# Reciprocal square roots on GpSimd's power operation, outside layer 1

## The chip, the cores and the metric

The kernel runs on one core of a Trainium2 chip. The metric is the device time of one execution in microseconds. A core has five engines, each with a queue of its own that is worked through in order: PE (TensorE, matrix products; PEld is its loading of weights), DVE (VectorE), ACT (ScalarE, which applies functions by table), POOL (GpSimd) and SP (SyncE, which here issues most DMAs). Engines meet only at semaphores and at the data in the on-chip memories.

## The reference

The input x is one image of 256 channels by 64 x 64 pixels in float32, that is 4096 tokens of 256 channels. Four layers follow each other, each a residual on x.

- Layer 0: group norm without scale, then linear attention over sliding windows with 8 heads of 32 channels: q and k are sigmoids, v is divided by its norm, and the sums over three windows are divided by q times the windowed k.
- Layer 1: group norm, then a deformable 3 x 3 convolution with a layer norm, offsets and masks.
- Layer 2: layer norm, then causal gated linear attention in which k and v are divided by their norms; then layer norm and a mixture of 8 experts, two for each token.
- Layer 3: layer norm, softmax attention of all 4096 tokens with each other; then layer norm and a mixture of 8 wider experts, two for each token.

The lines that the change bears on are the norms:

```python
v = v / jnp.maximum(jnp.linalg.norm(v, axis=1, keepdims=True), 1e-12)   # layer 0

def _l2_normalize(x, axis=-1):                                          # layer 2: k and v
    n = jnp.sqrt(jnp.sum(x * x, axis=axis, keepdims=True))
    return x / jnp.maximum(n, 1e-12)

def _ln_t(v, eps=1e-5):                                                 # layers 2 and 3, attention and experts
    m = jnp.mean(v, axis=-1, keepdims=True)
    s = jnp.var(v, axis=-1, keepdims=True)
    return (v - m) / jnp.sqrt(s + eps)
```

## The kernel before, in words

Tokens lie in 32 tiles of 128 (P = 128, NT = 32), four tiles to a block of 512 (TPB = 4, NB = 512, NBLK = 8 blocks). A framework for tiles puts the operations of each engine into an order of its own before the program runs, from its own estimates and the dependences, and places the semaphores. Only the tensor engine's order in the main part of layer 0 is written out by hand. Buffers come from pools and rotate.

An inverse norm is made the same way everywhere: a small tile of sums of squares or of variances gets a floor or an epsilon added on VectorE, then ScalarE takes the square root in place, then VectorE the reciprocal in place. ScalarE evaluates a function from a table, and a function that is not in the table at hand has an ACT_TABLE_LOAD in front of it, which the profile counts to the line of the function. There are these places:

- `layer_norm` (L188): statistics of up to four tiles (L195, L196), L198 adds epsilon, L199 and L200 are the square root and the reciprocal on 128 x 4 elements (`ln_rstd`), and L208 applies it on VectorE; with `on_act` ScalarE does. It is called by `attn2_project` (L1151), by `route` (L1594) and by layer 3's first stage (L1886).
- `project0` (L345): the projections of layer 0. It runs for each half of the channels. The products for q and k come first; then, for each of 8 blocks, products for k and v (in PSUM, `l_kv_ps`), a sigmoid for k on ScalarE (L367), a square of v (L369), the sum over each head's 32 channels (L370), the floor (L371), the square root and reciprocal of 128 x 16 elements `l_ss` (L372, L373), the product with v (L376), and the states k times v (L144, `l_S_ps`), copied out by L382. After a half, `sums0` (L384) adds the states over windows on POOL, and `norms0` (L403) computes the windowed k times q on VectorE (L429 to L437) with one product for each step on PE (L439). The scheduler mixes the steps of `norms0` with the next half's blocks.
- `attn2_project` (L1142): for each of 8 blocks, `layer_norm`, transposes (`to_channels`, L217), the products for q, k and v, a product q times k on POOL (L1163), the squares of k and v on ScalarE (L1170) with the sums on VectorE (L1171), the floor (L1172), the square root and the reciprocal of 128 x 64 elements `a_ss` (L1173, L1174), the product with v on VectorE (L1175) and with k on POOL (L1176), then transposes of v and the products for the gate. Most of its buffers exist once (`bufs=1`).
- `attn2_sum` (L1278): the causal sums of layer 2, two tiles at a time, with the masks (L1307) on VectorE and the products L1332 on PE. Between them run the steps of `route` (L1585) for the block before: `layer_norm`, the addition and a copy on POOL (L1596, L1597), the logits, the choice of two experts (L1579 is the exponential of its softmax), the places of the tokens in the experts' lists (L1633 to L1636), and eight indirect DMAs on POOL's queue that scatter the rows (L1639).
- Layer 3's attention: a stage of norms for all blocks (L1886), which waits for the gathered results of the experts of layer 2; then, for each block of queries, 32 tiles of keys with scores, an exponential (L1938) and products with v (L1943), and one step of `route` after every fourth tile of keys.
- `rstd` (L146) for group norms and for layer 1, and a general path of layer 2 (L1426) that is not executed on these inputs.

Of the kernel before, what the change touches and what calls it, by code (L numbers as in the profile page):

```python
# [10 lines left out]
F32 = mybir.dt.float32  # L11
BF16 = mybir.dt.bfloat16
I32 = mybir.dt.int32
AF = mybir.ActivationFunctionType
ALU = mybir.AluOpType
# [4 lines left out]
P = 128  # L20
# [58 lines left out]
def bc(ap, axis, n):  # L79

    ap = ap.unsqueeze(axis)
    shape = list(ap.shape)
    shape[axis] = n
    return ap.to_broadcast(shape)


class Net:
# [6 lines left out]
    def constants(self, pool):  # L94
        nc = self.nc
        self.ident = pool.tile([P, P], F32, tag="ident", name="ident")
        make_identity(nc, self.ident)
        self.ones_row = pool.tile([1, P], F32, tag="ones_row", name="ones_row")
        nc.gpsimd.memset(self.ones_row, 1.0)
        self.one = pool.tile([P, 1], F32, tag="one", name="one")  # L100
        nc.gpsimd.memset(self.one, 1.0)
        self.ones_col = self.one

        self.flags = pool.tile([P, 3], F32, tag="flags", name="flags")
        self.mom = pool.tile([P, 2, 2], F32, tag="mom", name="mom")

        self.grp = pool.tile([P, 16, 8], F32, tag="grp", name="grp")
        nc.gpsimd.memset(self.grp, 0.125)
        nc.gpsimd.affine_select(out=self.grp, in_=self.grp, pattern=[[-8, 16], [0, 8]], base=0,
                                channel_multiplier=1, compare_op=ALU.is_ge, fill=0.0)  # L110
        nc.gpsimd.affine_select(out=self.grp, in_=self.grp, pattern=[[8, 16], [0, 8]], base=7,
                                channel_multiplier=-1, compare_op=ALU.is_ge, fill=0.0)
        self.pp = pool.tile([P, NPP], F32, tag="pp", name="pp")
        nc.sync.dma_start(out=self.pp, in_=self.A["pp"])
# [31 lines left out]
    def rstd(self, pool, var, eps, tag):  # L146
# [5 lines left out]
        nc.vector.reciprocal(r, r)  # L152
        return r

    def group_norm(self, x, dst):


        nc, tc = self.nc, self.tc
        with tc.tile_pool(name="gn", bufs=1) as pool:
            mv = pool.tile([P, 2, 2], F32, tag="mv", name="gn_mv")  # L160
            for m in range(2):
                st = pool.tile([P, NBLK, 6], F32, tag=f"st{m}", name="gn_st")
                for j in range(NBLK):
                    nc.vector.bn_stats(st[:, j, :], x[:, m, j * NB : (j + 1) * NB])
                nc.vector.bn_aggr(mv[:, m, :], st)
            mean, r = self.group_scale(pool, mv)
            for m in range(2):
                for out, src in dst(m):
                    nc.vector.tensor_scalar(out, src, mean[:, m : m + 1], r[:, m : m + 1], ALU.subtract, ALU.mult)
# [18 lines left out]
    def layer_norm(self, pool, x, out, eps, on_act=False):  # L188

        nc = self.nc  # L190
        n = x.shape[1]
        st = pool.tile([P, TPB, 6], F32, tag="ln_st", name="ln_st")[:, :n]
        mv = pool.tile([P, TPB, 2], F32, tag="ln_mv", name="ln_mv")[:, :n]
        for i in range(n):
            nc.vector.bn_stats(st[:, i, :], x[:, i, :])  # L195
            nc.vector.bn_aggr(mv[:, i, :], st[:, i, :])  # L196
        r = pool.tile([P, TPB], F32, tag="ln_rstd", name="ln_rstd")[:, :n]
        nc.vector.tensor_scalar_add(r, mv[:, :, 1], eps)  # L198
        nc.scalar.activation(r, r, AF.Sqrt)  # L199
        nc.vector.reciprocal(r, r)  # L200
        if on_act:
            shift = pool.tile([P, TPB], F32, tag="ln_shift", name="ln_shift")[:, :n]
            nc.vector.scalar_tensor_tensor(shift, mv[:, :, 0], -1.0, r, ALU.mult, ALU.mult)
        for i in range(n):
            if on_act:
                nc.scalar.activation(out[:, i, :], x[:, i, :], AF.Identity, bias=shift[:, i : i + 1], scale=r[:, i : i + 1])
            else:
                nc.vector.tensor_scalar(out[:, i, :], x[:, i, :], mv[:, i, 0:1], r[:, i : i + 1], ALU.subtract, ALU.mult)  # L208
# [136 lines left out]
    def project0(self, hf, y, q, k, v, S, wp, ps):  # L345

        nc, w = self.nc, self.w
        for dst, base in ((q, 0), (k, C)):
            cols = slice(base + hf * P, base + hf * P + P)
            for nb in range(NBLK):  # L350
                p = ps.tile([P, NB], F32, tag="qk", name="l0_qk_ps")
                self.mm(p, [(w["w_qk0"][:, kt, cols], y[:, kt, nb * NB : (nb + 1) * NB]) for kt in range(2)])
                nc.scalar.activation(dst[:, nb * NB : (nb + 1) * NB], p, AF.Sigmoid)
        cols = slice(hf * 2 * P, (hf + 1) * 2 * P)
        for nb in range(NBLK):
            ts = slice(nb * TPB, (nb + 1) * TPB)
            kt4 = wp.tile([P, TPB, P], F32, tag="kt", name="l0_kt")
            ss = wp.tile([P, TPB, 4], F32, tag="ss", name="l0_ss")
            sq = wp.tile([P, TPB, 4, D], F32, tag="sq", name="l0_sq")
            ps_v = []  # L360
            for i in range(0, TPB, 2):
                p = ps.tile([P, 2, 2, P], F32, tag="kv", name="l0_kv_ps", bufs=4)
                for j in range(2):
                    t = nb * TPB + i + j
                    self.mm(p[:, j].rearrange("p a c -> p (a c)"),
                            [(y[:, kt, t * P : (t + 1) * P], w["w_kv0"][:, kt, cols]) for kt in range(2)])
                nc.scalar.activation(kt4[:, i : i + 2, :], p[:, :, 0, :], AF.Sigmoid)  # L367
                ps_v.append(p[:, :, 1, :].rearrange("p t (h c) -> p t h c", c=D))
                nc.scalar.activation(sq[:, i : i + 2], ps_v[-1], AF.Square)  # L369
            nc.vector.tensor_reduce(ss, sq, AX.X, ALU.add)  # L370
            nc.vector.tensor_scalar_max(ss, ss, 1e-24)  # L371
            nc.scalar.activation(ss, ss, AF.Sqrt)  # L372
            nc.vector.reciprocal(ss, ss)  # L373
            for i, p in zip(range(0, TPB, 2), ps_v):
                vs = v[:, nb * TPB + i : nb * TPB + i + 2, :].rearrange("p t (h c) -> p t h c", c=D)
                nc.vector.tensor_mul(vs, p, bc(ss[:, i : i + 2], 3, D))  # L376
            p = ps.tile([P, TPB, P], F32, tag="S", name="l0_S_ps", bufs=1)
            for i in range(TPB):
                self.mm(p[:, i, :], [(kt4[:, i, :], v[:, nb * TPB + i, :])])
            for h in range(4):  # L380
                hp = slice(h * D, (h + 1) * D)
                (nc.scalar.copy if h % 2 else nc.vector.tensor_copy)(S[hp, ts, :], p[hp, :, hp])  # L382
# [759 lines left out]
    def attn2_project(self, b, t, A, wg_bd, wp, ps):  # L1142

        nc, w = self.nc, self.w
# [22 lines left out]
        ss = wp.tile([P, 2, TPB, NH], F32, tag="ss", name="a2_ss")  # L1167
# [2 lines left out]
            nc.scalar.activation(sq, x, AF.Square)  # L1170
            nc.vector.tensor_reduce(ss[:, j], heads(sq), AX.X, ALU.add)  # L1171
        nc.vector.tensor_scalar_max(ss, ss, 1e-24)  # L1172
        nc.scalar.activation(ss, ss, AF.Sqrt)  # L1173
        nc.vector.reciprocal(ss, ss)  # L1174
        nc.vector.tensor_mul(heads(v), heads(v), bc(ss[:, 1], 3, D))  # L1175
        nc.gpsimd.tensor_tensor(heads(k), heads(k), bc(ss[:, 0], 3, D), ALU.mult)  # L1176
        vT = A["vT"][:, :, b * NB : (b + 1) * NB]
# [202 lines left out]
    def attn2_chunks(self, t, ctxt, sim, gate):  # L1380

        nc, tc, w, A = self.nc, self.tc, self.w, self.A
        with (
# [16 lines left out]
            for b in range(NBLK):  # L1400
# [21 lines left out]
                ss = wp.tile([P, TPB, 2 * NH], F32, tag="ss", name="a2_ss")  # L1422
                nc.vector.tensor_reduce(ss, heads(sq), AX.X, ALU.add)
                nc.vector.tensor_scalar_max(ss, ss, 1e-24)
                nc.scalar.activation(ss, ss, AF.Sqrt)
                nc.vector.reciprocal(ss, ss)  # L1426
                nc.vector.tensor_mul(heads(kv), heads(kv), bc(ss, 3, D))

                qT = wp.tile([P, 2, NB], F32, tag="qT", name="a2_qT")
# [776 lines left out]
```

## Time and profile before

| | us |
|---|---|
| median of three runs | 4277.86 |
| the three runs | 4275.56, 4277.86, 4278.22 |
| the profiled execution | 4303.36 |
| its span, first to last instruction | 4301.6 |
| layer 0, projections (65 to 230) | 165 |
| layer 2, projections (2000 to 2240) | 240 |
| layer 2, sums with routes (2280 to 2600) | 320 |
| layer 3, attention (2760 to 3710) | 950 |

The span is one execution as the hardware profiler recorded it, and all times of single instructions come from it. In the timeline's rows a start and a duration in microseconds are followed by the engine, the line, the operation, what is written and read, and in brackets how long the engine had stood idle before it and whose work ended that. In the rows of groups the busy time in microseconds and the mean of one instruction in nanoseconds stand after the first bar, and the idle time before them after the second. The mean granted clock of TensorE in this execution is 0.917 of full speed. The profile has 104 ACT_TABLE_LOAD instructions of 1283 ns each.

### The profile page before, as it was taken

To read this page: it belongs to the slowest core of one execution; us is meant where nothing else is said; L and a number is where in the kernel's file an instruction comes from. 1 tells how busy PE (TensorE), PEld (TensorE's weight loads), DVE (VectorE), ACT (ScalarE), POOL (GpSimd) and SP (SyncE) were. 2 spreads that over 40 slices of the span, in tenths; PEclk is the share of its full clock that TensorE was granted. 3 is DMA by queue.
4 is the path that set the end of the run, shared out by engine and by line. 5 is a ranking of instruction groups with operands and counts; after the bars stand their busy time and mean duration, and the time that the engine had idled before them with its cause. 6 is when DMAs were issued, how large, how long until landed. Compare 5 with 4: busy or idle time off the path is not lost.

```text
span 4301.6 us, 55879 instructions
## 1 busy us (share of the span) xinstructions
PE 3561.6 (83%) x21872; PEld 2318.2 (54%) x21872; DVE 1731.6 (40%) x3780; ACT 1254.4 (29%) x2172; POOL 1459.4 (34%) x1376
## 2 busy tenths in 40 slices
PE   7867888888877676675658779799999999899997
PEld 4412333322332465564436557566666668688886
DVE  6865445555554355455655555501001111211111
ACT  5423232333332353431111123322122222233331
POOL 1167776676775134433333334000000001011110
PEclk9989999999998888887768879899999999899999
DMA  1003313301001411110000157200000000355454
GB/s 49 2 25 103 111 58 92 95 21 35 19 23 67 120 54 45 44 54 16 0 0 21 40 169 251 87 0 10 10 11 10 11 5 16 118 191 196 182 203 167
DMA packets 137783, 294.00 MB, mean 68 GB/s; under 512 B 14817, under 2 KB 72802, under 8 KB 128290
## 3 DMA queue, kind: packets, MB, share of 16 engines
q1 hardware_dynamic: 113138, 234.80, 16.6%
q0 software_dynamic: 13056, 35.93, 2.2%
q10 hardware_dynamic: 11312, 19.55, 1.3%
q8 instruction: 177, 2.90, 0.3%
q14 instruction: 100, 0.82, 0.1%
HBM read 202.53 MB, written 87.70 MB: 67 GB/s over the span
## 4 chain that ended last, share of the span: by engine, by line
PE 33%; issue 11%; DVE 4%; DMA 3%; POOL 2%; ACT 1%; another core or an unknown queue 0%; SPq 0%; POOLq 0%; ACTq 0%; DVEq 0%
PE a_o_ps L1943 10%; PE a_s_ps L144 10%; PE f_h_ps L144 2%; PE a_qkv_ps L144 2%; PE f_y_ps L144 2%; POOL ys L1780 2%; DMA ys<-f_y,f_at 1%; PE a_q_ps L144 1%; PE a_o_ps L144 1%; DMA f_g<-ys 1%; PE tr_ps L217 1%; PE a_c_ps L1332 1%; DVE a_sm L1307 1%; PE a_u_ps L144 1%; PE a_st_ps L144 0%
## 5 line engine op out<-in xcount | busy, mean ns | idle before, releaser
L561 POOL TENSOR_TENSOR l_sm<-l_sc,mask 128x512 f32<-128x512 f32 (+3 forms) x624 | 783.8, 1275 | 285.4 <-ACT l_sc L555 278.2
L561 DVE TENSOR_TENSOR l_sm<-l_s,mask 128x512 f32<-128x512 f32 (+3 forms) x624 | 451.7, 747 | 475.2 <-PE l_s L547 472.9
L547 PE MATMUL l_s<-l_q,l_k 32*128 32x384 f32 (+2 forms) x3584 | 420.8, 538 | 199.1 <-DVE l_sm L561 187.6
L555 ACT COPY l_sc<-l_s 128x512 f32<-128x512 f32 (+3 forms) x448 | 339.0, 757 | 755.7 <-PE l_s L547 725.5
L1943 PE MATMUL a_o_ps<-a_v,a_e 128*128 128x257 f32 x2048 | 489.4, 380 | 0.0
L144 PE MATMUL a_s_ps<-a_qT,a_nT 128*128 128x512 f32 (+1 forms) x1152 | 487.8, 546 | 0.0
L1943 PEld LDWEIGHTS a_o_ps<-a_v,a_e 128*128 128x128 f32 x2048 | 388.9, 190 | 147.3 <-issue 104.1
L547 PEld LDWEIGHTS l_s<-l_q,l_k 32*128 32x128 f32 x3584 | 152.9, 192 | 464.6 <-DVE l_sm L561 276.1
L1639 POOL DMA_INDIRECT xs<-f_n,f_to x64 | 62.4, 976 | 883.9 <-DVE f_to L1636 841.1
L1938 ACT ACTIVATE a_e<-a_s_ps 128x512 f32<-128x512 f32 (+1 forms) x288 | 158.0, 549 | 687.4 <-PE a_s_ps L144 666.0
L144 PE MATMUL f_h_ps<-f_xT,f_w 128*128 128x256 f32 x1440 | 344.0, 387 | 11.9 <-DVE f_xT L1743 3.5
L1780 POOL DMA_INDIRECT ys<-f_y,f_at x144 | 139.6, 970 | 567.2 <-ACT f_y L1779 541.4
L144 PE MATMUL f_y_ps<-f_w,f_h 128*128 128x256 f32 x1440 | 328.1, 379 | 0.0
L144 PEld LDWEIGHTS f_h_ps<-f_xT,f_w 128*128 128x128 f32 x1440 | 265.0, 191 | 79.8 <-ACT f_h L1753 16.5
L852 PE MATMUL l_acc_ps<-ident,l_pr 128*128 128x128 f32 x1600 | 207.2, 290 | 118.7 <-DVE l_pr L848 114.3
L144 PEld LDWEIGHTS a_s_ps<-a_qT,a_nT 128*128 128x128 f32 x1152 | 216.3, 190 | 129.9 <-issue 112.9
L144 PEld LDWEIGHTS f_y_ps<-f_w,f_h 128*128 128x128 f32 x1440 | 268.2, 190 | 33.7
L852 PEld LDWEIGHTS l_acc_ps<-ident,l_pr 128*128 128x128 f32 x1600 | 192.2, 150 | 133.4 <-DVE l_pr L848 126.3
L848 DVE TENSOR_TENSOR l_pr<-l_vk,l_w_ps 128x1280 f32<-128x1280 f32 x128 | 182.2, 1480 | 90.0 <-ACT l_w_ps L837 80.1
L1753 ACT ACTIVATE f_h<-f_h_ps,f_w 128x256 f32<-128x256 f32 x360 | 163.7, 468 | 132.0 <-PE f_h_ps L144 129.2
L588 PE MATMUL l_a_ps<-l_sm,l_v 128*32 128x512 f32 (+3 forms) x1408 | 174.3, 565 | 0.5 <-POOL l_sm L561 0.5
L588 PE MATMUL l_b_ps<-l_sm,l_v 128*32 128x256 f32 (+2 forms) x2176 | 169.4, 383 | 0.3 <-POOL l_sm L561 0.3
(441 smaller groups left out, 4388.4 us busy)
## 6 DMA issues: line engine op xcount, KB each, us to landing
f_w<-in_f_w SPq DMA_DIRECT2D x36, 1152.0 KB
f_w<-in_f_w SPq DMA_DIRECT2D x36, 1028.0 KB
xs<-zero SPq DMA_DIRECT2D x8, 4160.0 KB
l_vk<-vt SPq DMA_DIRECT2D x180, 128.0 KB
f_x<-xs SPq DMA_DIRECT2D x72, 260.0 KB
f_w<-in_f_w SPq DMA_DIRECT2D x36, 384.0 KB
l_rcp<-l_recd SPq DMA_DIRECT2D x48, 256.0 KB
f_w<-in_f_w SPq DMA_DIRECT2D x36, 257.0 KB
```

The costliest lines, as they stand in the source:

```text
L144: self.nc.tensor.matmul(out, lhsT, rhs, start=(i == 0), stop=(i == len(pairs) - 1))
L547: nc.tensor.matmul(s[pair][:, j], k[hp, key * P : (key + 1) * P], qs[hp], start=True, stop=True)
L555: nc.scalar.copy(src, s[pair])
L561: eng.tensor_tensor(to, part[:, :, which, :], bc(mask, 1, 2), ALU.mult)
L588: nc.tensor.matmul(out, v[:, key, hp], sms[pair][:, j, base + lo * wide : base + hi * wide], start=not seen[nm], stop=(left[nm] == 0 and h ...
L848: nc.vector.tensor_tensor(pr, vk, bc(wps[:, j, dy], 3, D), ALU.mult)
L852: nc.tensor.matmul(acc[:, m, j, :], pf[:, dx, m * P : (m + 1) * P], self.ident, is_transpose=True, start=(j == 0 and dy == 0 and dx == 0 a ...
L1639: nc.gpsimd.indirect_dma_start(out=self.xs_parts[(2 * (t0 + i) + r) % (4 * TPB)], in_=n[:, i, :], in_offset=None, out_offset=bass.Indirect ...
L1753: nc.scalar.activation(h[:, m, :], q, AF.Gelu, bias=w1[:, 2 * hidden + m : 2 * hidden + m + 1])
L1780: nc.gpsimd.indirect_dma_start(out=self.ys_parts[(i % 4) * NI + k], in_=y[:, k, :], in_offset=None, out_offset=bass.IndirectOffsetOnAxis(a ...
L1938: nc.scalar.activation(e, p, AF.Exp, scale=1.0 / 16.0)
L1943: nc.tensor.matmul(o[i][:, : C + 1], e[:, i * P : (i + 1) * P], v[:, j, :], start=(j == 0), stop=(j == NT - 1))
```

## The change

The pair of square root and reciprocal becomes one operation on GpSimd, the power with exponent -0.5, on the same tile and in place. The exponent comes from a constant of one element for each partition, read with a stride of zero. It is used in `layer_norm`, `project0`, `attn2_project` and the general path; `rstd` stays as it was. Line numbers in the changed kernel are a few higher from here on; the power is its line 159.

```diff
-        self.one = pool.tile([P, 1], F32, tag="one", name="one")
-        nc.gpsimd.memset(self.one, 1.0)
+        pair = pool.tile([P, 2], F32, tag="one", name="one")
+        nc.gpsimd.memset(pair[:, 0:1], 1.0)
+        nc.gpsimd.memset(pair[:, 1:2], -0.5)
+        self.one, self.mhalf = pair[:, 0:1], pair[:, 1:2]
...
+    def rsqrt(self, a):
+
+        self.nc.gpsimd.tensor_tensor(a, a, self.mhalf.to_broadcast(list(a.shape)), ALU.pow)
...
@@ layer_norm
         nc.vector.tensor_scalar_add(r, mv[:, :, 1], eps)
-        nc.scalar.activation(r, r, AF.Sqrt)
-        nc.vector.reciprocal(r, r)
+        self.rsqrt(r)
...
@@ project0, and in the same way attn2_project and the general path
             nc.vector.tensor_scalar_max(ss, ss, 1e-24)
-            nc.scalar.activation(ss, ss, AF.Sqrt)
-            nc.vector.reciprocal(ss, ss)
+            self.rsqrt(ss)
```

More of the change, by code (lines that the diff above doesn't have):

```diff
@@ L1172, in attn2_project @@
         nc.vector.tensor_scalar_max(ss, ss, 1e-24)
-        nc.scalar.activation(ss, ss, AF.Sqrt)
-        nc.vector.reciprocal(ss, ss)
+        self.rsqrt(ss)
         nc.vector.tensor_mul(heads(v), heads(v), bc(ss[:, 1], 3, D))
@@ L1424, in attn2_chunks @@
                 nc.vector.tensor_scalar_max(ss, ss, 1e-24)
-                nc.scalar.activation(ss, ss, AF.Sqrt)
-                nc.vector.reciprocal(ss, ss)
+                self.rsqrt(ss)
                 nc.vector.tensor_mul(heads(kv), heads(kv), bc(ss, 3, D))
```

## The prediction

> **What bounds the kernel now.** I read the page's busy shares and its chain of waits first, then the groups of ScalarE by shape, then busy time by stage for the stages that hold one of the edited places, then the timeline around one instance of each, on all engines.
>
> The page (engine, busy us, share, instructions; then the chain that ended last):
> ```profile
> PE 3561.6 (83%) x21872; PEld 2318.2 (54%) x21872; DVE 1731.6 (40%) x3780; ACT 1254.4 (29%) x2172; POOL 1459.4 (34%) x1376
> ...
> PE 33%; issue 11%; DVE 4%; DMA 3%; POOL 2%; ACT 1%; another core or an unknown queue 0%; SPq 0%; POOLq 0%; ACTq 0%; DVEq 0%
> ```
> TensorE is the bound over the whole; ScalarE ends 1% of the chain, POOL 2%. Unloading ScalarE is worth little, unless its work lies inside a serial chain. Groups of ScalarE by shape (count, then busy us, mean ns, then idle before):
> ```profile
> L199 ACT ACT_TABLE_LOAD x19 | 24.4, 1283 | 24.2 <-DMA f_g<-ys 16.4 <-issue 4.5 <-DMA a_ked<-in_kvn_ed 3.0
> ...
> L372 ACT ACT_TABLE_LOAD x15 | 19.2, 1283 | 0.3
> ```
> The sigmoid that follows L372, at L367, reloads its own table 13 times. Each square root needs a table that its neighbours (sigmoid, exp, gelu) do not, so most cost a load before and one after. Stages, in this order: layer 0's projections, layer 2's projections, layer 2's sums with the routes between them, layer 3's attention:
> ```profile
> core 0: us, PE busy (x) PEld busy (x) DVE busy (x) ACT busy (x) POOL busy (x), PEclk, DMA share, GB/s
> 65.00:230.00 165.00, 138.31 (x495) 76.24 (x493) 145.69 (x271) 91.26 (x199) 32.88 (x19) 0.93 0.01 2
> 2000.00:2240.00 240.00, 143.55 (x520) 99.62 (x520) 148.95 (x318) 33.72 (x58) 76.45 (x41) 0.76 0.01 3
> 2280.00:2600.00 320.00, 247.65 (x1770) 194.41 (x1771) 177.62 (x647) 71.36 (x136) 108.39 (x107) 0.79 0.28 93
> 2760.00:3710.00 950.00, 942.30 (x3509) 647.90 (x3507) 100.95 (x435) 202.95 (x354) 59.63 (x67) 1.00 0.03 9
> ```
> In layer 3, PE is busy 942 of 950 us: what changes on ScalarE there shows nowhere. In layer 2's projections no engine is busy over 62%: a serial chain sets the time, and the edit lies in it:
> ```profile
> 2029.81 0.20 DVE L1172 TENSOR_SCALAR a_ss<-a_ss 128x64 f32<-128x64 f32 x1
> 2030.04 0.26 ACT L1173 ACTIVATE a_ss<-a_ss 128x64 f32<-128x64 f32 x1 [1.51 <-DVE a_ss L1172]
> 2030.33 0.55 DVE L1174 RECIPROCAL a_ss<-a_ss 128x64 f32<-128x64 f32 x1 [0.32 <-ACT a_ss L1173]
> 2030.92 1.23 DVE L1175 TENSOR_TENSOR a_v<-a_v,a_ss 128x1024 f32<-128x1024 f32 x1
> 2031.03 2.89 POOL L1176 TENSOR_TENSOR a_qk<-a_qk,a_ss 128x1024 f32<-128x1024 f32 x1 [5.97 <-DVE a_ss L1174]
> ```
> No load stands here (the last function before was a square), so only 0.91 us (2030.01 to 2030.92) can be removed per block.
>
> **What goes.** By the changed program's order of instructions, 57 square roots (16 of 128x16 at 0.22 us, 8 of 128x64 at 0.26, 33 of 128x4 or less at 0.21: 12.5 us of ACT), 57 reciprocals (16 x 0.25 + 8 x 0.55 + 33 x 0.18 = 14.3 us of DVE) and 63 table loads (all at L199, L372 and L367, eight each at the softmax of the router and layer 3's exponential, and a few others: 63 x 1.283 = 81 us of ACT). SP's queue keeps its order; the tensor engine's count stays. ALU.pow enters POOL 57 times (line 159 of the changed kernel): 8 of 64 elements a partition, 16 of 16, 33 of 4 or 2.
>
> **The price of a power.** No row has one. Low end: POOL's TENSOR_TENSOR at 128x160 takes 519 ns and at 128x288 793 ns, 2.1 ns an element over some 0.17 us: 0.31, 0.20 and 0.18 us for 64, 16 and 4. A power is no single step, however. The nearest non-elementary row is DVE's reciprocal: 3.35 us for 96x512 is 6.5 ns an element, five to six times DVE's plain multiplication (1.23 us for 1024 elements, 1.2 ns each). Six times POOL's 2.1 is 13 ns for one such step; a power is about three (a logarithm, a product, an exponential): 40 ns an element, 2.7, 0.8 and 0.33 us. I take this, an estimate. High end: the elements of 16 partitions one by one, 16 x 13 = 211 ns an element, 13.7 us for 64.
>
> **Layer 2's projections** (8 blocks of 27.2 us). The path between L1172 and L1175 turns from 0.91 us into a power plus two changes of engine. DVE to POOL in the rows above is 0.15 us (2030.88 to 2031.03) and back I take 0.05: 8 x (2.7 + 0.2 - 0.91) = +16 us. Behind the waiting multiplication L1175, DVE queues the transposes' copies and the products; PE waits for L1175 9.7 us at a time already, so nothing covers this. With the low end it is 8 x (0.31 + 0.2 - 0.91) = -3; with the high end +104. The norm's power of 128x4 stands in POOL's order ahead of the product q times k, and replaces 0.6 us of chain by 0.5.
>
> **Layer 0's projections** (16 blocks, 5.5 us of PE each). The block's chain loses at least a load. ACT around one instance:
> ```profile
> 65.75 1.28 ACT L372 ACT_TABLE_LOAD   x1
> 67.05 0.22 ACT L372 ACTIVATE l_ss<-l_ss 128x16 f32<-128x16 f32 x1
> 67.28 1.28 ACT L367 ACT_TABLE_LOAD   x1
> 68.57 0.38 ACT L367 ACTIVATE l_kt<-l_kv_ps 128x256 f32<-128x256 f32 x1
> ```
> The first load runs ahead of its input, so the 1.3 us is on the chain only in part: DVE waits for the square root 5.3 us in all, PE for the normalised v 9.8. POOL is idle while the blocks run (its window sums, 22 us each, follow a half's last block). The sum of the two waits, 15 us, is the most that can go; PE at 138 of 165 us lets little of it through, and the new order puts five or six steps of the window norms (DVE, L429 to L437 at 0.68, 0.91, 0.59 and 0.87 us: 3 us a step) behind the last block instead of between blocks, where POOL's window sums stretch some DVE instructions (0.27 us becomes 1.88). I take -3, with -14 and +10 as ends.
>
> **The routes in layer 2's sums** (8). Here POOL's queue matters. The scheduler places the next route's power behind the eight scatters of the present one, 8 x 1.28 = 10.2 us:
> ```profile
> 2336.61 0.18 DVE L200 RECIPROCAL ln_rstd<-ln_rstd 128x4 f32<-128x4 f32 x1 [1.79 <-ACT ln_rstd L199]
> ...
> 2341.27 0.96 POOL L1639 DMA_INDIRECT xs<-a_qk,f_to  x1 [0.30 <-issue]
> ...
> 2342.31 1.22 DVE L1307 TENSOR_TENSOR a_sm<-a_s,tri 128x1024 f32<-128x1024 f32 x1 [3.22 <-remote]
> ```
> The square root came at 2336.6, the power could start at 2342.2 and end at 2342.6. DVE's four L208 wait for it, and both masks L1307 stand behind them, for which PE's products wait. DVE already stalls to 2342.31, so the loss is the work that no longer fits ahead (one mask and three L208, 0.4 + 1.2 + 0.7 us, and the power): 2.9 us. The new order also pulls the matmul of the counts forward, which makes the scatters some 2.5 us earlier: 8 x (2.9 - 2.5) = +3. Ends: -7 (the wait for the table, 8 x 0.9) and +23 (no earlier scatters).
>
> **The rest.** Layer 3's norms ahead of attention wait for gathered rows (16.4 us of idle time at L199), and inside attention PE covers all. At the seams (first block, last route before the experts) a load and a half is on the path: -2, ends -4 and 0.
>
> Sum: 16 - 3 + 3 - 2 = +14 us on the profiled execution's 4303.36 us (span 4301.6 plus 1.8): 4317. That execution lies 25.5 us above the median 4277.86, at a clock of 0.917, so against the median the ratio 1.0033 gives 4291.
>
> **Pages weighed.** Layer 0's trace shows a 1.28 us load and the next activation 0.02 us behind it. The Trainium skill's "ScalarE: Activation LUTs" (What ACT_TABLE_LOAD costs) has a switch at about 2.7 us with a drain; by that the 63 would be 168 us of ACT, not 81, and this case's rows show no such drain. Its "GPSIMD Engine Reference" (Engine selection) advises against elementwise work on GpSimd, about two times slower for two inputs; by that alone a power of 64 would stay well below the time I take, and the projections would gain; the page has no price for a power.
>
> **The rivals.** All turn on one unknown, the power of 64 elements, and on the place where it is paid. (A) A quick power, at most 0.75 us: the projections of layer 2 end between -3 and 0, layer 0's gain -5 with powers of 0.2 us, the routes -2, the seams -2: some -12 with the low end, 4266. For it: POOL's low fixed time, and the idle POOL beside all blocks. Against it: the reciprocal's factor of six on DVE. It decides below 0.75 us, where the projections no longer lose and the other three alone make 9 us. (B) 0.75 to 2.0 us: 0 to +10 in the projections, less 2 to 9 elsewhere, about even: 4278. (C) My forecast, 2.0 to 6 us: (2.0 - 0.71) x 8 = +10 to +42 there, less 2: 4287 to 4318. (D) Beyond 6 us: over +42 there, and layer 0's 16 powers (over 1.6 us each, in a chain of 5.5 us a block) and the routes come on top: +60 to +140, 4338 to 4418. (E) The change does less than it says, and loads come back elsewhere: the new order leaves 41 of 104, so no.
>
> **How the numbers follow.** What a measurement of this kernel can tell from no change is about 0.2%, 8.6 us. A 0.22, B 0.26, C 0.40, D 0.12. C is likeliest; its own range is 4286 to 4316. The range from A's middle (-14, where layer 0 gives its most) to the lower part of D (+67) leaves out two in ten: 4264 to 4345. Faster is A, same is B, slower C and D.
>
> **What would show it.** Rows of line 159 on POOL at three shapes (2.7, 0.8, 0.33 us); the distance between the maximum and the product with v in layer 2 (0.91 before, 2.9 after); the block period there (27.2 before, 29.2 after) and in layer 0; the route's power ending behind the eighth scatter; 41 loads; PE unchanged in layer 3. I am wrong if the power takes under 1 us or over 6, if the window sums catch layer 0's powers, or if the routes delay layer 2's sums by more than 3 us each.

## The result and the profile after

The changed kernel takes 4433.88 us (median of four runs, 4431.36 to 4438.53) against 4277.18 for the kernel before: a ratio of 1.0368, with an interval of 1.035 to 1.0386. It is 157 us slower. The prediction had said slower, but by 13 us, and 4433.88 lies far above its range.

The page of the changed kernel (engine, busy us, share and instructions; then the chain that ended last):

```profile
PE 3574.9 (81%) x21872; PEld 2324.3 (52%) x21872; DVE 1710.6 (39%) x3723; ACT 1166.8 (26%) x2052; POOL 1628.2 (37%) x1434
...
PE 31%; issue 13%; POOL 5%; DVE 2%; DMA 2%; ACT 0%; SPq 0%; POOLq 0%; DVEq 0%; ACTq 0%
```

ACT lost 88 us and 63 table loads, as the change promises; POOL gained 169 us with 58 more instructions (57 powers and a memset), and its share of the chain that ended last rose from 2% to 5%. The groups of POOL by shape say what a power costs (count, then busy us and mean ns, then idle before):

```profile
L159 POOL TENSOR_TENSOR a_ss<-a_ss,one 128x64 f32<-128x64 f32 x8 | 84.2, 10524 | 40.2 <-DVE a_ss L1176 40.2
L159 POOL TENSOR_TENSOR l_ss<-l_ss,one 128x16 f32<-128x16 f32 x16 | 50.5, 3156 | 114.2 <-DVE l_ss L376 114.2
L159 POOL TENSOR_TENSOR ln_rstd<-ln_rstd,one 128x4 f32<-128x4 f32 x31 | 33.6, 1084 | 394.4 <-DVE ln_rstd L204 394.3
```

The shortest of each size are 10.52, 2.90 and 1.01 us. The two larger sizes differ by 7.62 us for 48 elements: 0.159 us an element, with 0.36 us beside it. The forecast had 2.7, 0.8 and 0.33.

VectorE's waits in layer 2's projections of the changed kernel (us in total, times, longest):

```profile
DVE a_v L1178 <- POOL a_ss L159: 85.1, 8, 10.6
```

and the rows of one block there:

```profile
2107.80 0.19 DVE L1176 TENSOR_SCALAR a_ss<-a_ss 128x64 f32<-128x64 f32 x1
2108.07 10.52 POOL L159 TENSOR_TENSOR a_ss<-a_ss,one 128x64 f32<-128x64 f32 x1 [5.03 <-DVE a_ss L1176]
2118.62 1.23 DVE L1178 TENSOR_TENSOR a_v<-a_v,a_ss 128x1024 f32<-128x1024 f32 x1 [10.63 <-POOL a_ss L159]
```

The 0.91 us between the floor and the product with v has become 10.63, and nothing runs on VectorE meanwhile. In layer 0 a block looks the same, with the smaller power:

```profile
98.58 0.17 DVE L376 TENSOR_SCALAR l_ss<-l_ss 128x16 f32<-128x16 f32 x1
98.89 2.90 POOL L159 TENSOR_TENSOR l_ss<-l_ss,one 128x16 f32<-128x16 f32 x1 [8.30 <-DVE l_ss L376]
...
101.82 0.76 DVE L380 TENSOR_TENSOR l_v<-l_kv_ps,l_ss 128x256 f32<-128x256 f32 x2 [3.07 <-POOL l_ss L159]
```

Before, VectorE had work of the window norms between the floor and the product, and waited 5.3 us in all for the square root; now it waits 42.9 us for the power (the waits before, then after: us in total, times, longest):

```profile
DVE l_ss L373 <- ACT l_ss L372: 5.3, 6, 1.1
...
DVE l_v L380 <- POOL l_ss L159: 42.9, 16, 3.1
```

In layer 2's sums, the wait is at the routes:

```profile
DVE a_qk L213 <- POOL ln_rstd L159: 40.0, 7, 7.2
```

To see the stages I took the starts of the same instructions from each trace: the second reciprocal of the window norms, the first sum over heads of q times k (L1164 before the change) and the first mask in layer 2, the last mask, the first and last exponential of layer 3's attention, and the end. The kernel before was profiled a second time among the experiments; that is the better base, for a reason told there. Durations in us:

| stage | before | before, second profile | changed |
|---|---|---|---|
| layer 0 up to the window norms | 257.6 | 256.8 | 304.1 |
| rest of layer 0, layer 1 | 1767.5 | 1767.4 | 1763.4 |
| layer 2, projections | 230.1 | 230.1 | 302.9 |
| layer 2, sums with routes | 233.1 | 202.3 | 238.9 |
| layer 2's experts, layer 3's norms | 281.5 | 286.2 | 290.0 |
| layer 3, attention | 928.9 | 928.9 | 928.8 |
| layer 3's experts | 602.8 | 604.0 | 601.3 |
| span | 4301.6 | 4275.7 | 4429.4 |

Three stages carry the loss: 47, 73 and 37 us against the second profile. The other stages differ by 4 us at most, in both directions. Layer 3's attention does not move, although square roots and loads left it. Busy time in the changed kernel by stage, for layer 2's projections, layer 2's sums and layer 3's attention (us, then busy us and count of each engine, the granted clock, DMA share and GB/s):

```profile
2040.00:2360.00 320.00, 141.71 (x529) 96.35 (x529) 148.77 (x316) 32.89 (x47) 170.22 (x63) 0.71 0.02 5
2385.00:2635.00 250.00, 184.65 (x1539) 145.74 (x1539) 122.68 (x416) 28.43 (x61) 83.31 (x79) 0.76 0.10 34
2888.00:3838.00 950.00, 942.11 (x3512) 647.94 (x3512) 103.06 (x431) 178.36 (x327) 68.53 (x78) 1.00 0.03 9
```

In the projections PE and VectorE do the work of before, 142 and 149 us, in 320 us instead of 240, and POOL's busy time has gone from 76 to 170. In the attention ACT has lost 25 us, beside a PE that is busy for 942 of 950 as before.

### The profile page after: what moved, and what is told of

Read it like the earlier page. It is cut to its first block, busy times and chain, and to the rows that moved or that the text cites. A ratio compares the mean times of both kernels' runs of the same rounds, so it can differ in the third digit from the quotient of the medians.

```text
span 4429.4 us, 55780 instructions
## 1 busy us (share of the span) xinstructions
PE 3574.9 (81%) x21872; PEld 2324.3 (52%) x21872; DVE 1710.6 (39%) x3723; ACT 1166.8 (26%) x2052; POOL 1628.2 (37%) x1434
## 4 chain that ended last, share of the span: by engine, by line
PE 31%; issue 13%; POOL 5%; DVE 2%; DMA 2%; ACT 0%; SPq 0%; POOLq 0%; DVEq 0%; ACTq 0%
PE a_o_ps L1945 10%; PE a_s_ps L146 10%; PE f_h_ps L146 2%; PE a_qkv_ps L146 2%; POOL a_ss L159 2%; PE f_y_ps L146 2%; POOL ys L1782 2%; POOL xs L1641 1%; DMA ys<-f_y,f_at 1%; PE a_q_ps L146 1%; DMA f_g<-ys 1%; PE tr_ps L222 1%; PE a_u_ps L146 1%; PE a_c_ps L1335 0%; POOL ln_rstd L159 0%
## 5 line engine op out<-in xcount | busy, mean ns | idle before, releaser
L159 POOL TENSOR_TENSOR ln_rstd<-ln_rstd,one 128x4 f32<-128x4 f32 (+1 forms) x33 | 35.1, 1062 | 422.2 <-DVE ln_rstd L204 422.0
```

The lines of the kernel that those rows point to most:

```text
L159: self.nc.gpsimd.tensor_tensor(a, a, self.mhalf.to_broadcast(list(a.shape)), ALU.pow)
```

## The experiments

The theories were these. P: the power's own duration stands on the chain and makes the loss. O: the new order of instructions, above all the power's place in POOL's queue behind the scatters, makes a good part. The lines of the edits are those of the changed kernel unless said otherwise.

**A cheap operation in the power's place.** The kernel then leaves out the inverse norms: it multiplies by a constant near them, and its output is not the reference's. Every instruction keeps its place in the order of its engine; only the operation differs, but for two more memsets of constants at the start.

```diff
-        self.nc.gpsimd.tensor_tensor(a, a, self.mhalf.to_broadcast(list(a.shape)), ALU.pow)
+        self.nc.gpsimd.tensor_tensor(a, a, self.near[:, c : c + 1].to_broadcast(list(a.shape)), ALU.mult)
```

> The power is replaced by a multiplication with a constant on the same engine, the same tiles and in the same order of instructions on every engine; the constants are chosen near the true inverse norms, and the output is not the reference's. Theory P (the price of the power on the chain makes the loss): the 10.5, 3.2 and 1.0 us shrink to about 0.3, 0.2 and 0.2 us, the loss goes, and what is left is what the removed table loads and hops are worth, 4255 to 4280 us. Theory O (the new order of DVE's and PE's instructions, and the power's place behind the scatters, make a good part of the loss): 4310 us or more, with layer 0's first stage still 20 us or more longer than before.

It took 4319.18 us, ratio 1.0096 (1.008 to 1.0113). The groups of POOL by shape:

```profile
L162 POOL TENSOR_TENSOR ln_rstd<-ln_rstd,one 128x4 f32<-128x4 f32 x31 | 7.9, 255 | 396.0 <-DVE ln_rstd L207 395.8
L162 POOL TENSOR_TENSOR l_ss<-l_ss,one 128x16 f32<-128x16 f32 x16 | 7.8, 487 | 110.8 <-DVE l_ss L379 110.8
L162 POOL TENSOR_TENSOR a_ss<-a_ss,one 128x64 f32<-128x64 f32 x8 | 2.3, 293 | 40.2 <-DVE a_ss L1179 40.2
```

The multiplication of 64 elements takes 0.293 us, the power 36 times as long. The stages divide the theories: layer 0's first is 258.8 us (the second profile of before: 256.8) and layer 2's projections 221.5 (230.1), so in both the new order is innocent and the power's duration is the loss. But the sums are 231.1 against 202.3, with a norm operation of 0.26 us: there 29 us are lost to something other than duration. The total holds 24 us more, in layer 2's experts (310.2 for 286.2): 78 scatters of expert results run there instead of 72, and the last six end 26 us after the others. I put this down to the other norms, by which the tokens are routed otherwise, and not to the change. The total alone, within theory O's range, would have misled.

**One place at a time.** The power in layer 0's projections alone, in layer 2's alone, in the layer norms alone; the other places go back to the lines of before:

```diff
-        self.rsqrt(r)
+        nc.scalar.activation(r, r, AF.Sqrt)
+        nc.vector.reciprocal(r, r)
```

Layer 0 alone:

> The power in layer 0's projections alone, the square root and reciprocal elsewhere. Theory P: 16 powers of about 3.2 us in a chain in which the square root and reciprocal had cost 2 to 2.7 us with other DVE work beside them: +40 to +50 us, 4317 to 4327, the first product of layer 0's main part some 45 us later. Theory L (the loss belongs to layer 2's long power, and layer 0's is mostly an effect of the order): +5 to +20.

Layer 2's projections alone:

> The power in layer 2's projections alone. Theory P: 8 x (10.52 + 0.2 - 0.91) = +78, less what the next link had of slack: +70 to +80 us, 4347 to 4357. If the profiles of before and after, 127.8 us apart, hide a further part of the 157 us between the medians in this stage, up to +100.

The layer norms alone:

> The power in the layer norms alone (33 of 128x4 or 128x2). Theory P: about 1.0 us each, off the path in layer 2's projections, behind the scatters in the routes (+6 in the profiles), one hop of 0.9 us each in layer 3's norms (+2): +5 to +12 us, 4282 to 4289. If table loads had been on the path at these places: below 4277.

Against 4278.7 for the kernel before in this batch:

| power in | us | ratio, interval | stage that grew (second profile of before) |
|---|---|---|---|
| layer 0 | 4321.73 | 1.0104, 1.0087 to 1.0121 | layer 0 up to the window norms: 303.3 (256.8) |
| layer 2's projections | 4352.09 | 1.0176, 1.0159 to 1.0193 | projections: 303.9 (230.1) |
| the layer norms | 4317.71 | 1.0119, 1.0072 to 1.0167 | sums: 236.3 (202.3) |

The three excesses, 43, 73 and 39 us, add up to 155 of the 157. (The last is rough: one of the four executions of that run took 4355.98 us, the others 4314.79 to 4320.18.) The first two are what P expected. The third is not: 5 to 12 us were expected. The rows of one route of that run, VectorE and POOL:

```profile
2331.78 0.17 DVE L204 TENSOR_SCALAR ln_rstd<-ln_mv 128x4 f32<-128x4 f32 x1
...
2336.70 0.96 POOL L1643 DMA_INDIRECT xs<-a_qk,f_to  x1 [0.30 <-issue]
2337.69 1.05 POOL L159 TENSOR_TENSOR ln_rstd<-ln_rstd,one 128x4 f32<-128x4 f32 x1
2338.78 1.38 DVE L213 TENSOR_SCALAR a_qk<-t,ln_mv,ln_rstd 128x256 f32<-128x256 f32 x4 [6.82 <-POOL ln_rstd L159]
2340.07 2.35 DVE L1312 TENSOR_TENSOR a_sm<-a_s,tri 128x1024 f32<-128x1024 f32 x2
...
2341.35 0.64 PE L1337 MATMUL a_c_ps<-a_sm,a_qk 128*32 128x128 f32 x4 [6.74 <-DVE a_sm L1312]
```

The variance is ready at 2331.95. The power starts 5.7 us later, right behind the eighth scatter, VectorE stands idle 6.82 us, and both masks follow, for which PE has waited 6.74.

**The kernel before, once more**, and **the layer norms without the routes**. For the latter, `route` calls `layer_norm` with an argument that keeps the square root and the reciprocal there:

```diff
-        self.layer_norm(wp, t[:, tiles, :], n[:, :, :C], 1e-5)
+        self.layer_norm(wp, t[:, tiles, :], n[:, :, :C], 1e-5, power=False)
```

> The kernel before once more, for a second profile: its profiled execution lay 25.5 us above its median. Expected: a profiled execution within 5 us of 4277, and the 25 us found in one stage, or else spread over the whole as a lower clock.

> The power in the layer norms of layer 2's projections and of layer 3's first stage alone; the routes keep square root and reciprocal. Against the run with the power in all layer norms this shows what the place behind the scatters costs: theory P with the queue, 4 to 8 us less than that run; if the queue does not matter, the same within 2 us. The table loads at the routes come back, which layer 3's attention hides.

The second profile of the kernel before took 4277.4 us, and the 25.5 us that the first one had above the median are found: its sums took 233.1 us, those of the second 202.3 (layer 2's experts and layer 3's norms gave 4.7 back). The rows of one route in the second profile, VectorE and POOL:

```profile
2332.34 0.18 DVE L200 RECIPROCAL ln_rstd<-ln_rstd 128x4 f32<-128x4 f32 x1 [1.79 <-ACT ln_rstd L199]
...
2333.02 1.20 DVE L1307 TENSOR_TENSOR a_sm<-a_s,tri 128x1024 f32<-128x1024 f32 x1
...
2334.83 1.21 DVE L1307 TENSOR_TENSOR a_sm<-a_s,tri 128x1024 f32<-128x1024 f32 x1
...
2337.13 0.96 POOL L1639 DMA_INDIRECT xs<-a_qk,f_to  x1 [0.30 <-issue]
```

The second mask starts at 2334.83, while the scatters still run. In the prediction's rows of the first profile it stood still until 2342.31, after the last scatter, 3.22 us idle, and the first profile's waits have this "remote" (another core or an unknown queue) six times for 15.7 us:

```profile
DVE a_sm L1307 <- remote: 15.7, 6, 3.2
```

The second profile has none. What set the first execution apart was not found.

With the power only in the other layer norms the kernel takes 4274.62 us, ratio 0.9998 (0.9989 to 1.0007): no change, and 43 us less than with the routes, where 4 to 8 were expected. Its sums are 202.8 us. So the whole third part belongs to the routes.

**The scatters after the power.** To take the queue away without touching the power, a block's scatters were made to depend on the next block's inverse deviation, in the run with the power in the layer norms and, as a control, in the kernel before.

```diff
-        nc.vector.tensor_copy(S["to"][:, :, tiles], place)
...
+                nc.vector.tensor_scalar_mul(big, last[:, 0:1], 1e6)
+                nc.vector.tensor_scalar(S["to"][:, :, tiles], place, big, None, ALU.min)
```

> The power in the layer norms alone, as in the run that was 40 us slower than before, but the scatters of a block are issued only after the next block's power: the places' conversion to integers takes a minimum with a large multiple of the next block's inverse deviation, so that the scatters depend on it. Theory Q (the power waits behind eight scatters of 1.27 us in POOL's queue, and VectorE's norm and masks behind the power): layer 2's sums come back from 236 us to 203 to 210, the whole to 4280 to 4292. Theory S (what costs is the power on POOL as such, a change of engine in a chain that had none): sums of 225 us or more, 4305 or more.

> The same later scatters in the kernel before, with square root and reciprocal: the control for the run above. Both theories: sums within 5 us of 202, the whole 4270 to 4285; the difference of the two runs is then what the power costs in the layer norms when no scatter stands ahead of it, 0 to +10 by theory Q.

With the power: 4295.77 us, ratio 1.0041 (1.0027 to 1.0056), sums 222.7. The control: 4288.7, ratio 1.0029 (1.002 to 1.0039), sums 212.8, so the edit itself costs 11 us. VectorE's wait at the routes (us in total, times, longest), first with the scatters ahead of the power:

```profile
DVE a_qk L213 <- POOL ln_rstd L159: 43.8, 8, 7.2
```

then with the scatters behind it:

```profile
DVE a_qk L213 <- POOL ln_rstd L159: 9.7, 8, 1.2
```

Both runs missed the ranges given for theory Q, in the total and in the sums, since the control was not free. The difference from the control is what counts: 7 us in the whole, where the two intervals overlap, and 10 in the sums; it was 39 and 34 with the scatters ahead. At least some 24 of the 34 us in the sums are thus the queue. The other 10 need not be the power's either, for the edit's own minimum stands elsewhere in the two runs. With the power it is ahead of both masks on VectorE:

```profile
2325.90 1.38 DVE L213 TENSOR_SCALAR a_qk<-t,ln_mv,ln_rstd 128x256 f32<-128x256 f32 x4 [1.23 <-POOL ln_rstd L159]
...
2327.38 2.35 DVE L1649 TENSOR_SCALAR f_to<-f_place,f_big 128x8 int32<-128x8 f32 x1
2329.65 2.34 DVE L1313 TENSOR_TENSOR a_sm<-a_s,tri 128x1024 f32<-128x1024 f32 x2
```

and in the control behind them:

```profile
2331.61 1.22 DVE L1308 TENSOR_TENSOR a_sm<-a_s,tri 128x1024 f32<-128x1024 f32 x1
...
2333.46 2.32 DVE L1645 TENSOR_SCALAR f_to<-f_place,f_big 128x8 int32<-128x8 f32 x1
```

In these blocks the norm starts 1.23 us after the variance with the power and 2.08 us in the control, so the power's own time delays nothing here; the second mask starts about 6.1 us after it against 4.2, with 2.35 us of minimum ahead. A run with the minimum in the same place was not made.

**The price.** Two powers of 32 elements in place of one of 64:

```diff
-        self.rsqrt(ss)
+        self.rsqrt(ss[:, 1])
+        self.rsqrt(ss[:, 0])
```

> In layer 2's projections the power of 64 elements becomes two of 32, first the half for v, then the half for k; all else as in the changed kernel. If the price is linear in the elements (0.35 + 0.159 n us from the three sizes): each takes 5.4 us, the product with v waits 5.1 us less per block, and k's half runs beside v's transposes: about -35 to -41 us against the changed kernel, some 4395. If the price is mostly a fixed cost of the instruction: two of nearly 10 us, no gain or slower than 4434.

and two powers in a row, with 0.5 and -1:

```diff
-        self.rsqrt(ss)
+        for e in (self.half, self.minus):
+            nc.gpsimd.tensor_tensor(ss, ss, e.to_broadcast(list(ss.shape)), ALU.pow)
```

> In layer 2's projections two powers in a row, with exponents 0.5 and -1, in place of one with -0.5; the result is the same. Theory P: 8 more powers of 10.5 us wholly on the chain: +84 us on the changed kernel, 4518. If part of the power is hidden: less than +60. If the price depends on the exponent, the two differ from 10.52 us.

Their groups of POOL by shape, first the halves:

```profile
L159 POOL TENSOR_TENSOR a_ss<-a_ss,one 128x32 f32<-128x32 f32 x16 | 86.4, 5415 | 40.2 <-DVE a_ss L1176 40.2
```

then the two in a row:

```profile
L1181 POOL TENSOR_TENSOR a_ss<-a_ss,one 128x64 f32<-128x64 f32 x16 | 168.3, 10521 | 40.9 <-DVE a_ss L1179 40.2
```

The halves took 4397.53 us, ratio to the kernel before 1.0281 (1.0264 to 1.0297): 36 less than the changed kernel, and 5.4 us for 32 elements is what 0.36 + 0.159 x 32 gives. The pair took 4522.07, ratio 1.0572 (1.0555 to 1.0589): 88 more than the changed kernel, 11 for each added power of 10.52. All of a power's time counts in this stage, and its price goes by the number of elements, not by the exponent, as far as these three exponents show.

No version with the power was faster than the kernel before; the best is the one without it in the three places that wait, and it is equal to the kernel before.

## Why the prediction was right or wrong

**Wrong: the price of a power.** The prediction took 2.7 us for 64 elements, three steps of an assumed 13 ns. The rows show 10.52. The method of bounding held (0.31 to 13.7), but the value was taken from a ratio on another engine and a count of steps that no run shows; the measured one is near the high end. The Trainium skill's "GPSIMD Engine Reference" (Engine selection) warns of a factor of about two for two-input arithmetic. The two products with the inverse norms in the prediction's rows, of 128x1024 elements each, are near that: 1.23 us on VectorE, 2.89 on GpSimd. This case's multiplication of 64 elements at 0.293 us and power at 10.52 show that the choice of operation on this engine mattered far more here.

**Right in form, wrong in size: layer 2's projections.** The sum 8 x (power + 0.2 - 0.91) gives 78 us with 10.52; the stage grew by 73. No cover was found, as had been said. The missing 5 do not come from the power's length: with the multiplication the same sum gives -3, and the stage became 9 us shorter. Where they are saved was not looked for.

**Wrong: layer 0's projections.** The prediction gave -3, with -14 and +10 as ends, and those ends came from waits of before and from the order; the power's price was not in them. At the high end of that price a power of 16 elements is 3.5 us, and 16 of them are 57: the end had been on the page and was not carried into this term. Measured are 43 to 47 us. The rows show the wait: 42.9 us of VectorE behind 16 powers of 3.16 us. The suspected five or six moved steps of the window norms and the loads that went make together no more than 2 us: by so much is the stage longer with the multiplication.

**Right mechanism, wrong size: the routes.** That the power would stand behind eight scatters, and VectorE's norm and both masks behind the power, is what the rows show. But the loss was put at 2.9 us a route, because VectorE "already stalls to 2342.31". That stall was a mark of the one profiled execution. Without it the masks of before run beside the scatters, and the sums lose 34 us: 4.3 for each of eight routes, or 5.7 for each of the six that carry it, since the first has no scatters ahead and the last comes after the last mask. Against the first profile, from which the term was read, the changed kernel's sums are only 6 us longer (238.9 for 233.1), not far from the +3 of the term: the base was wrong. The scatters did come earlier: in those six routes the last one ends 4.9 to 6.1 us after the variance, against 7.3 to 7.6 in the second profile of before. The loss of 34 us stands with this already in it. The prediction had noted that its execution was 25.5 us above the median, carried the difference over as a ratio, and did not ask which stage held it; it was the stage that the term was read from.

**Not to be told: the seams.** The -2 of the rest has no counterpart that can be read: layer 2's experts and layer 3's norms took 290.0 us, and in the two profiles of before 281.5 and 286.2.

**Right:** layer 3's attention, at 928.9 and 928.8 us, and the 41 remaining table loads. The rival with a power beyond 6 us, +60 to +140 us, had the right mechanism; it was given a chance of 0.12, and even its upper end, 4418, is 16 us too low; the routes' own end was +23, and they lost 37 in the changed kernel.

## What to carry to other kernels

A function that moves to an engine on which it has no row in the trace is an unknown price, and the far end of that price must be carried into every term that holds it, not into the largest alone. An engine that looks idle on average may have a burst of DMA issues standing in its queue at just the moment that a short operation on a chain comes to it: here an operation of 0.26 us cost 29 us in layer 2's sums, and one of 1 us 34. When the profiled execution is longer than the median, find the stage that holds the difference before using any of its stalls as cover.

## What the runs showed that was not expected

- GpSimd's power costs 0.159 us for each element of a partition, with about 0.36 us beside it, at 2, 4, 16, 32 and 64 elements on 128 partitions (0.73, 1.01, 2.90, 5.42 and 10.52 us); the multiplication of 64 elements takes 0.293.
- In some places the smaller powers are longer: 2.90 to 3.73 us for 16 elements, 1.01 to 1.85 for 4. The power of 64 varied by 0.01 us only. What lengthens them was not tried.
- Taking 63 table loads of 1.283 us, 81 us of ScalarE, out of the program gained nearly nothing even with a cheap operation in their place: with the multiplication layer 0's first stage, which lost 29 loads, was 2 us longer in the new order, and layer 3's attention, which lost 16, 0.1 us shorter. Only layer 2's projections gained, 9 us, and no load had stood between their first sum and the end of their last block.
- The sums of the same program took 233.1 us in one execution and 202.3 in another, with VectorE's masks held until the last scatter in the first. The cause is open.
